# A scan's side work in other slots, and narrower state sums with turned keys in a linear attention

## The chip, the cores and the metric

The kernel runs on one core of one Trainium2 chip. The metric is the device time of one launch in microseconds (us), the median of three runs. One further execution of the same program was taken with the hardware profiler.

## The reference

The kernel computes a four-layer network over 32 sequences of 256 tokens with 128 features (8192 rows). Each layer is an attention-like part and a feed-forward part, both with adaptive layer norm (scale, shift and gate per sequence). Two parts matter here.

Layer 0, a selective scan in two branches (forward and "backward" convolution weights), for the normalized input h:

```python
u = softplus(conv(proj(LN(h))))            # one u per branch
delta = softplus(dt_W @ (deltaBC_W[:64] @ u) + dt_b)
B, C = rows 64..79 and 80..95 of deltaBC_W @ u
h_t = exp(delta_t * A) * h_{t-1} + (delta_t * u_t) * B_t      # 16 states per feature
y_t = sum over states of h_t * C_t, + u_t * D                 # both branches, times silu(proj)
```

Layer 1, an attention with 16 heads of 8 features: a local window of 64 tokens with softmax, and five causal linear attentions (the plain keys and values, and four levels with block means of 2, 4, 8 and 16 tokens), each divided by its normalizer:

```python
phi(x) = elu(x) + 1
out_t = sum over s <= t of phi(q_t) . phi(k_s) v_s / max(sum over s <= t of phi(q_t) . phi(k_s), 1e-6)
```

A gate mixes local and global outputs. Before this part, the routed feed-forward output of layer 0 has to be gathered by token and added to the residual x.

## The kernel before, in words

**Tiles and stages.** `x` stays in SBUF, transposed, as 16 tiles of 128 features by 512 tokens (two sequences). The stages run one after the other: modulation, `scan_layer`, the routed feed-forward of layer 0, `hale` (the attention of layer 1), and five more. Only `scan_layer` and `hale` differ in this change.

**What sets the order.** TensorE's instructions keep the order in which they are written (`mm`, `tr`, L386 and L390), and in the scan ScalarE's do too (`act`, L393, with `strict_act`). VectorE and GpSimd are ordered when the kernel is built, by a scheduler with its own costs; after that each engine takes its queue strictly in that order. What the text calls the built order is the order in which the instructions of the built program stand on an engine.

**The scan.** `scan_layer` writes an agenda of slots. Step p has slots 2p and 2p+1, a tile has eight steps (two branches of four groups of four states), and a tile b has T = 16b. In the first slot, `scan_even` writes 16 products into `dB` (four PSUM banks, one buffer), four scans `hs` on VectorE (L847), the second half of the weighing of step p-2 (products into `y`), the transposes of the first half of step p-1 into `hT`, and two decays (ScalarE exponentials) for step p+1. In the second slot, `scan_odd` has the transposes and the weighing of the other half and two more decays. ScalarE copies every `hT` to `hsT`. All other products and transposes of a tile share the one PSUM bank `tp`: two norms (`norm_rows`, `norm_out`), the projection, the products for u and delta, the rows of B and C (`scan_rows`, with two DMAs on SyncE that turn C through DRAM), the turning of delta times u (`scan_turn`), and the output's turn (`scan_end`). After `scan_end` comes `residual` (L533, two VectorE operations), which waits for two GpSimd products (L912, L913).

**Softplus.** `soft_start` reads a product from PSUM twice: ScalarE makes m = |v + bias|, VectorE r = max(v + bias, 0). `soft_end` makes log(1 + exp(-m)) on ScalarE, and GpSimd adds r. m and r have one buffer each. A tile has four of them (u and delta of both branches).

**The attention of layer 1.** `hale_slots` writes an agenda with 16 slots for a sequence q (T = 16q), which overlaps three sequences. The slots T to T+5 hold the window's six score blocks, T+6 to T+15 the ten blocks of the five linear attentions: scores into `S` (`hale_scores`), a causal mask on VectorE for one half (L1888) and on ScalarE and GpSimd for the other (L1890, L1891), and one slot later the products with the values (`hale_weighted`) into `po`. The second half of a sequence also takes the state of the first half, `kvs`: the sum of keys times values over 128 tokens. `hale_states` makes it by a product of `kt` (keys of the first half, tokens on partitions) with the values (`vzb`, `vzl`; 16 columns for each head: 8 features, then 8 of ones) and a mask for equal heads. `kt` comes from products of its own (a third part of `hale_values`, the key columns in `hale_level_values`) and its own `phi`; the same features, with tokens on the free axis, come from `hale_features` and `hale_level_keys` into `f`. These share three `tp` buffers with the rest.

**The gather.** For a tile that is needed in slot T of an even sequence, `gather_rows` writes eight indirect DMAs on GpSimd's queue (L1239) in slot T-48 and `gather_add` the weighted sums `gy` (L1261, L1262), four transposes and the residual in slot T-38. `got` and `gy` have one buffer.

Of the kernel before, what the change touches and what calls it, by code (L numbers as in the profile page):

```python
# [24 lines left out]
AF = mybir.ActivationFunctionType  # L25
ALU = mybir.AluOpType
# [4 lines left out]
P = 128  # L31
# [144 lines left out]
def packs(d):  # L176

    out = {}
# [40 lines left out]
    k.add("Wv", g["Wv"])  # L219
    k.add("vvk", np.concatenate([g["Wv"].T, g["Wvl"].T, by_heads(g["Wk"].T, DENSE)], 1))  # L220
    k.add("haar_Wk", np.stack([by_heads(diag_blocks(g["haar_Wk"][lvl].T, 16), DENSE) for lvl in range(4)], 1))
# [88 lines left out]
class Program:  # L310
# [326 lines left out]
    def scan_layer(self, w):  # L637
# [7 lines left out]
        with ExitStack() as ctx:  # L645
# [28 lines left out]
            for b in range(NB):  # L674
                a = s[b] = {"b": b}
                T = 16 * b
                put(T, self.clear_regions)

                for o, n, src in ((T - 40, 1, lambda a: self.x[a["b"]]), (T - 32, 2, lambda a: a["h"])):
                    put(o, lambda a, n=n, src=src: a.update({("st", n): self.norm_rows(src(a), self.nc.gpsimd)}), a)  # L680
                    put(o + 1, lambda a, n=n: self.scan_roots(a, n), a)
                    put(o + 3, lambda a, n=n: self.norm_scale(a["st", n][0], *a["r", n]), a)
                put(T - 36, self.scan_norm_out, a)
                put(T - 28, self.scan_norm_out2, s, a)
                put(T - 23, self.scan_proj, s, a)
                put(T - 22, self.scan_gate, s, a)
                put(T - 21, self.scan_gate2, s, a)
                for br in (0, 1):
                    o = T + 8 * br
                    put(o - 18, self.scan_u, s, a, br)  # L690
                    put(o - 17, self.scan_u2, s, a, br)
                    put(o - 15 + br, self.scan_delta, s, a, br)
                    put(o - 14 + br, self.scan_rows, s, a, br)
                    put(o - 11, self.scan_turn, s, a, br)
                    put(o - 9, self.scan_b, s, a, br)
                    put(o - 5, self.scan_c, s, a, br)
                put(T + 18, self.scan_sum, s, a)
                put(T + 19, self.scan_end, s, a)
            for t in sorted(agenda):
# [34 lines left out]
    def soft_start(self, src, bias):  # L734

        m, r = self.wk("sp_m"), self.wk("sp_r")
        self.act(m, src, AF.Abs, bias=bias)
        self.nc.vector.tensor_scalar(r, src, bias, 0.0, ALU.add, ALU.max)
        return m, r

    def soft_end(self, out, m, r):
        self.act(m, m, AF.Exp, scale=-1.0)
        self.act(m, m, AF.Ln, bias=1.0)
        self.nc.gpsimd.tensor_tensor(out, m, r, ALU.add)
# [83 lines left out]
    def scan_even(self, s, p):  # L828

        nc = self.nc  # L830
        if 0 <= p < 8 * NB:
# [13 lines left out]
            for n in range(4):  # L845
                decay = s["decay"][(4 * p + n) % 10].rearrange("p s t -> p (s t)")
                nc.vector.tensor_tensor_scan(hs[:, :, n], decay, dB[:, :, n], 0.0, ALU.mult, ALU.add)  # L847
        self.scan_weigh(s, p - 2, 1)
        self.scan_turned(s, p - 1, 0)
        self.scan_decay(s, p + 1, 0)  # L850

    def scan_odd(self, s, p):
# [46 lines left out]
    def scan_end(self, s, a):  # L899
        nc = self.nc  # L900
        py = self.ps("tp", (P, 4, P))
        for i in range(4):
            self.tr(py[:, i, :], a["yT"][:, i, :])
        y = self.wk("y")
        cut = dict(i=4, r=32)
# [7 lines left out]
        nc.gpsimd.tensor_tensor(y, y, a["h"], ALU.add)  # L913
        self.residual(0, 0, a["b"], y)

# [317 lines left out]

    def gather_rows(self, b):

        got = self.wk("got", (P, 4, 2, P))
        for t in range(4):
            for k in (0, 1):
# [7 lines left out]
                )  # L1246
        self.gather[b] = got

# [295 lines left out]
    def hale(self, w):  # L1544
        nc, c = self.nc, self.c
        BF = mybir.dt.bfloat16
        with ExitStack() as ctx:
# [17 lines left out]
            nc.vector.tensor_copy(self.locb[1], c.locq1)  # L1565
            self.kvs = wk("kvs", (P, 5, SEQ))
            self.kt = wk("kt", (P, 5, P))

# [20 lines left out]
    def hale_slots(self, w):  # L1589
# [9 lines left out]
        for q in range(2 * NB):  # L1599
# [3 lines left out]
            if s == 0:  # L1603
                tiles[b] = {}
                if self.gather:
                    put(side, T - 48, lambda b=b: self.gather_rows(b))
                    put(side, T - 38, lambda b=b: self.gather_add(0, b))
                put(side, T - 32, lambda t=tiles[b], b=b: t.update(xn=self.norm_in(self.x[b])))
                put(side, T - 30, lambda t=tiles[b], b=b: t.update(h=self.norm_out(t["xn"], self.ada_mods(1, 0, b), "h")))
# [18 lines left out]
            put(side, T - 4, lambda a=a: self.hale_features(w, a))  # L1628
            put(side, T - 3, lambda a=a: self.hale_level_values(a, 0, 0))
            put(side, T - 2, lambda a=a: self.hale_level_keys(a, 0))  # L1630
            put(side, T - 2, lambda a=a: self.hale_states(a, (0, 1)))
            put(side, T + 0, lambda a=a: self.hale_level_keys(a, 1))
            put(side, T + 1, lambda a=a: self.hale_level_values(a, 0, 1))
            put(side, T + 2, lambda a=a: self.hale_level_values(a, 1, None))
            put(side, T + 3, lambda a=a: self.hale_states(a, (2, 3)))
            put(side, T + 4, lambda a=a: self.hale_states(a, (4,)))
            for n in range(5):
# [169 lines left out]
    def hale_values(self, w, a, t):  # L1807

        n = 3 if t == 0 else 2
        pv = self.ps("tp", (P, n, P))  # L1810
        self.mm(pv, a["h"][:, t * P : (t + 1) * P], w.vvk[:, 0 : n * P])
        self.nc.vector.tensor_copy(
            self.vzb[t][:, :, :, 0:8], pv[:, 0:2, :].rearrange("p n (h d) -> p n h d", d=8)
        )
        if t == 0:
            self.phi(self.kt[:, 0, :], pv[:, 2, :])

    def hale_level_values(self, a, t, pair):

        if t == 0:  # L1820
            pv = self.ps("tp", (P, 2, 2, P))
            for l in (0, 1):
                lvl = 2 * pair + l
                self.mm(pv[:, l], a["hm"][:, lvl, 0:P], self.wl[:, lvl])
            lv = slice(2 * pair, 2 * pair + 2)
            src = pv[:, :, 1, :]
            self.phi(self.kt[:, 1 + 2 * pair : 3 + 2 * pair, :], pv[:, :, 0, :])
        else:
            src = self.ps("tp", (P, 4, P))
            for lvl in range(4):  # L1830
                self.mm(src[:, lvl, :], a["hm"][:, lvl, P:], self.wl[:, lvl, 1, :])
            lv = slice(0, 4)
        self.nc.vector.tensor_copy(self.vzl[t][:, lv, :, 0:8], src.rearrange("p l (h d) -> p l h d", d=8))

# [26 lines left out]
    def hale_states(self, a, ns):  # L1861

        pk = self.ps("tp", (P, len(ns), SEQ))
        for m, n in enumerate(ns):
            self.mm(pk[:, m, :], self.kt[:, n, :], self.set_values(n, 0)[:, :, 0:16])
        self.nc.vector.tensor_tensor(
            self.kvs[:, ns[0] : ns[-1] + 1, :],
            pk,
            self.c.same.unsqueeze(1).to_broadcast([P, len(ns), SEQ]),
            ALU.mult,  # L1870
        )
# [929 lines left out]
```

## Time and profile before

| | us |
|---|---|
| median of 3 runs (6840.84 to 6861.61) | 6856.3 |
| profiled execution | 6756.19 |
| its span, first to last instruction | 6754.3 |
| busy in the span: TensorE | 5907.4 |
| VectorE | 4350.0 |
| ScalarE | 3557.5 |
| GpSimd | 2660.5 |
| from the first to the last scan instruction (125 to 1144) | 1019 |
| attention of layer 1, first to last score product (1804 to 3826) | 2022 |

The profile is of one execution. In its rows PE is TensorE, PEld its weight loads (which overlap), DVE VectorE, ACT ScalarE, POOL GpSimd, SP SyncE. A row names line, engine and operation, what is written from what, the shape (partitions x elements), and a count; in square brackets a timeline gives the engine's idle time before the row and what ended it. An fp32 product shows as two matmul instructions, called passes here. Lines of helpers (L386, L390, L393, L533) stand for many callers, so one goes by the names of the tiles.

### The profile page before, as it was taken

How to read it: one execution, taken by the hardware profiler on the slowest of the kernel's cores; microseconds unless marked ns; L12 is line 12 of the kernel's file. 1: busy time of each engine (PE TensorE's matmuls, PEld its weight loads, DVE VectorE, ACT ScalarE, POOL GpSimd, SP SyncE). 2: the span in 40 equal slices, each digit the busy share in tenths (PEclk: the TensorE clock that was granted, in tenths of full speed). 3: DMA queues.
4: the chain of work that ended last, by engine and by line, in shares of the span. 5: the costliest groups of instructions: out<-in, count | busy, mean ns of one | idle time of the engine just before them, and what ended most of it. 6: DMA issues, size and time to landing. Idle time of an engine off the chain costs nothing. (4 is left out here: it accounts for less than half of the span.)

```text
span 6754.3 us, 132930 instructions
## 1 busy us (share of the span) xinstructions
PE 5907.4 (87%) x54209; PEld 3313.6 (49%) x54209; DVE 4350.0 (64%) x10025; ACT 3557.5 (53%) x5227; POOL 2660.5 (39%) x2881
## 2 busy tenths in 40 slices
PE   5777776899899999999999887999889998999987
PEld 3555555457555555555566444454422222444444
DVE  3666766621466666666666572888677774777779
ACT  5888885233344444444445442444478886544532
POOL 3555553566444444444444362444244543000000
PEclk7999998899899999999999877999999998989988
DMA  1101101135100000000000101111133442000010
GB/s 60 41 28 41 41 29 36 41 109 134 28 7 5 5 5 8 5 5 8 5 2 2 45 4 38 25 27 28 31 84 90 92 91 48 15 18 18 18 33 30
DMA packets 175447, 232.27 MB, mean 34 GB/s; under 512 B 46519, under 2 KB 95919, under 8 KB 174450
## 3 DMA queue, kind: packets, MB, share of 16 engines
q1 hardware_dynamic: 120656, 124.47, 7.3%
q0 software_dynamic: 26992, 56.62, 3.6%
q10 hardware_dynamic: 27186, 42.67, 1.7%
q8 instruction: 426, 6.98, 0.4%
q14 instruction: 187, 1.53, 0.1%
HBM read 88.28 MB, written 74.97 MB: 24 GB/s over the span
## 5 line engine op out<-in xcount | busy, mean ns | idle before, releaser
L1416 ACT ACTIVATE E<-S 128x1024 f32<-128x1024 f32 x448 | 459.0, 1025 | 592.8 <-PE S L386 579.4
L847 DVE TENSOR_TENSOR_SCAN hs<-decay,dB 128x512 f32<-128x512 f32 x512 | 583.1, 1203 | 196.9 <-PE dB L386 114.7
L298 DVE TENSOR_REDUCE mt<-S 128x4 f32<-128x1024 f32 (+1 forms) x512 | 550.2, 1088 | 224.5 <-PE S L386 223.8
L386 PE MATMUL S<-qa,kx 32*128 32x256 f32 x4096 | 556.2, 392 | 59.6 <-DVE mt L298 59.1
L393 ACT ACTIVATE hid<-S,bigw 128x1024 f32<-128x1024 f32 x512 | 537.6, 1112 | 124.2 <-PE S L386 124.0
L1888 DVE TENSOR_TENSOR E<-S,cst 128x1024 f32<-128x1024 f32 x320 | 391.2, 1223 | 301.1 <-PE S L386 300.5
L1891 POOL TENSOR_SCALAR_AFFINE_SELECT E<-E 128x1024 f32<-128x1024 f32 x320 | 350.2, 1094 | 594.6 <-ACT E L1890 594.2
L386 PE MATMUL S<-kx,q 32*128 32x512 f32 (+1 forms) x2048 | 540.4, 623 | 17.1 <-ACT kx L1534 16.1
L1890 ACT COPY E<-S 128x1024 f32<-128x1024 f32 x320 | 323.7, 1012 | 315.1 <-PE S L386 315.1
L2440 POOL TENSOR_TENSOR acc<-acc,ye 128x512 f32<-128x512 f32 x256 | 344.7, 1347 | 360.4 <-DVE ye L298 318.1
L386 PEld LDWEIGHTS S<-qa,kx 32*128 32x128 f32 x4096 | 350.8, 195 | 174.6 <-DVE mt L298 137.1
L1713 DVE TENSOR_REDUCE mt<-S 128x4 f32<-128x512 f32 (+1 forms) x256 | 205.2, 823 | 294.0 <-PE S L386 293.8
L386 PE MATMUL S<-qG,f 32*128 32x512 f32 x2560 | 382.3, 657 | 7.5 <-DVE E L1888 6.4
L386 PE MATMUL S<-hm,bigw 32*128 32x512 f32 x2048 | 338.7, 654 | 25.2 <-ACT hid L393 25.2
L393 ACT ACTIVATE hsT<-hT 128x1024 f32<-128x1024 f32 x256 | 260.4, 1017 | 179.7 <-PE hT L390 179.4
L390 PE MATMUL hT<-cst,hs 128*128 128x128 f32 x2048 | 285.9, 283 | 75.4 <-ACT hsT L393 73.5
L393 ACT ACTIVATE decay<-dl,A 128x510 f32<-128x510 f32 x512 | 339.2, 714 | 0.0
L386 PE MATMUL po<-E,vzl 128*32 128x128 f32 x8192 | 284.1, 279 | 50.1 <-POOL E L1891 50.1
L1760 ACT ACTIVATE E<-S 128x768 f32<-128x768 f32 (+1 forms) x192 | 169.1, 881 | 280.7 <-PE S L386 279.9
L390 PEld LDWEIGHTS hT<-cst,hs 128*128 128x128 f32 x2048 | 225.1, 143 | 169.6 <-ACT hsT L393 139.7
L386 PE MATMUL po<-E,vz 128*32 128x256 f32 x4096 | 300.2, 379 | 7.2 <-POOL E L1420 6.9
L386 PE MATMUL po<-hid,bigw 128*32 128x512 f32 x2048 | 277.2, 613 | 30.4 <-DVE ye L298 30.4
(520 smaller groups left out, 13307.8 us busy)
## 6 DMA issues: line engine op xcount, KB each, us to landing
gb<-gT SPq DMA_DIRECT2D x256, 256.0 KB
regions<-zeros ACTq DMA_DIRECT2D x16, 2048.0 KB
rx<-far SPq DMA_DIRECT2D x64, 256.0 KB
expert_rows<-eo SPq DMA_DIRECT2D x39, 256.0 KB
out<-out SPq DMA_DIRECT2D x16, 256.0 KB
xTd<-xT SPq DMA_DIRECT2D x15, 256.0 KB
xT<-xTd SPq DMA_DIRECT2D x15, 256.0 KB
bigw<-in_s SPq DMA_DIRECT2D x10, 256.0 KB
```

What stands on the lines that cost most here:

```text
L298: return lambda *args, **kw: self.tc.keep_in_program_order(op(*args, **kw))
L386: return self.tc.keep_in_program_order(self.nc.tensor.matmul(out, lhsT, rhs, start=start, stop=stop, **kw))
L390: return self.tc.keep_in_program_order(self.nc.tensor.transpose(out, in_, self.c.ident[:k, :k]))
L393: ins = self.nc.scalar.activation(*args, **kw)
L847: nc.vector.tensor_tensor_scan(hs[:, :, n], decay, dB[:, :, n], 0.0, ALU.mult, ALU.add)
L1416: nc.scalar.activation(e, src, AF.Exp, scale=scale)
L1713: nc.vector.tensor_reduce(m.rearrange("p (g j) -> p g j", j=2), pm[:, :, x] if i == 0 else pm[:, :, :, 0:192], AX.X, ALU.max, negate=True,)
L1760: nc.scalar.activation(e, src, AF.Exp, scale=1.0 / math.sqrt(8))
L1888: nc.vector.tensor_tensor(e, src, self.c.caus.unsqueeze(1).to_broadcast([P, 8, P]), ALU.mult)
L1890: nc.scalar.copy(e, src)
L1891: nc.gpsimd.affine_select(e, e, [[0, 8], [1, P]], ALU.is_ge, 0.0, base=0, channel_multiplier=-1)
L2440: nc.gpsimd.tensor_tensor(a["acc"], a["acc"], ye, ALU.add)
```

## The change

It has four parts.

1. *Scan, slots.* The four softplus products (`scan_u`, `scan_delta`, for both branches) go to the second slots of steps, with the other users of `tp` placed around them: norms four slots earlier, projection and gate two later, u in slots T-19 and T-13 (was T-18 and T-10), delta in T-15 and T-7 (was T-15 and T-6), the rows in T-14 and T-6, the turn one later, the output two later. The residual leaves `scan_end` and is written in slot T+23 (was T+19). In `scan_even` the transposes and decays come ahead of the weighing.
2. *Scan, softplus.* m no longer comes from ScalarE's Abs: VectorE makes m = v - 2r from r and the product, and ScalarE's Exp adds the bias, so that m + bias = -|v + bias|.
3. *Attention, keys and states.* `kt` is no longer computed from products and `phi`: `hale_turn_keys` transposes the features `f` of the first half (five transposes in two groups, with a ScalarE copy each). The state sums take 9 columns of each head (8 features and one of ones) instead of 16, 144 for 256, in groups of three and two, later. `kvs` is cleared once at the start. The level values of both halves are now made the same way, four products of 128 columns each. The weights lose the key columns.
4. *Gather.* In this stage the rows are fetched in quarters (two DMAs each) in slots T-62, T-58, T-54 and T-50, summed in quarters in T-52 to T-40, and finished in T-38.

```diff
-                for o, n, src in ((T - 40, 1, ...x), (T - 32, 2, ...h)):
+                for o, n, src in ((T - 44, 1, ...x), (T - 36, 2, ...h)):
...
-                put(T - 36, self.scan_norm_out, a)
-                put(T - 28, self.scan_norm_out2, s, a)
-                put(T - 23, self.scan_proj, s, a)
-                put(T - 22, self.scan_gate, s, a)
-                put(T - 21, self.scan_gate2, s, a)
+                put(T - 40, self.scan_norm_out, a)
+                put(T - 32, self.scan_norm_out2, s, a)
+                put(T - 21, self.scan_proj, s, a)
+                put(T - 20, self.scan_gate, s, a)
+                put(T - 19, self.scan_gate2, s, a)
                 for br in (0, 1):
                     o = T + 8 * br
-                    put(o - 18, self.scan_u, s, a, br)
-                    put(o - 17, self.scan_u2, s, a, br)
-                    put(o - 15 + br, self.scan_delta, s, a, br)
-                    put(o - 14 + br, self.scan_rows, s, a, br)
-                    put(o - 11, self.scan_turn, s, a, br)
+                    put(T - 19 + 6 * br, self.scan_u, s, a, br)
+                    put(T - 18 + 6 * br, self.scan_u2, s, a, br)
+                    put(o - 15, self.scan_delta, s, a, br)
+                    put(o - 14, self.scan_rows, s, a, br)
+                    put(o - 10, self.scan_turn, s, a, br)
...
-                put(T + 19, self.scan_end, s, a)
+                put(T + 21, self.scan_end, s, a)
+                put(T + 23, lambda a: self.residual(0, 0, a["b"], a["y"]), a)
...
-        self.act(m, src, AF.Abs, bias=bias)
         self.nc.vector.tensor_scalar(r, src, bias, 0.0, ALU.add, ALU.max)
-        return m, r
+        self.nc.vector.scalar_tensor_tensor(m, r, -2.0, src, ALU.mult, ALU.add)
+        return m, r, bias
-    def soft_end(self, out, m, r):
-        self.act(m, m, AF.Exp, scale=-1.0)
+    def soft_end(self, out, m, r, bias):
+        self.act(m, m, AF.Exp, bias=bias)
...
-        self.scan_weigh(s, p - 2, 1)
         self.scan_turned(s, p - 1, 0)
         self.scan_decay(s, p + 1, 0)
+        self.scan_weigh(s, p - 2, 1)
...
-                    put(side, T - 48, lambda b=b: self.gather_rows(b))
-                    put(side, T - 38, lambda b=b: self.gather_add(0, b))
+                    for t in range(4):
+                        put(side, T - 62 + 4 * t, lambda b=b, t=t: self.gather_rows(b, (t,)))
+                        put(side, T - 52 + 4 * t, lambda b=b, t=t: self.gather_sum(b, (t,)))
+                    put(side, T - 38, lambda b=b: self.gather_end(0, b))
...
-            put(side, T - 3, lambda a=a: self.hale_level_values(a, 0, 0))
-            put(side, T - 2, lambda a=a: self.hale_level_keys(a, 0))
-            put(side, T - 2, lambda a=a: self.hale_states(a, (0, 1)))
-            put(side, T + 0, lambda a=a: self.hale_level_keys(a, 1))
-            put(side, T + 1, lambda a=a: self.hale_level_values(a, 0, 1))
-            put(side, T + 2, lambda a=a: self.hale_level_values(a, 1, None))
-            put(side, T + 3, lambda a=a: self.hale_states(a, (2, 3)))
-            put(side, T + 4, lambda a=a: self.hale_states(a, (4,)))
+            put(side, T - 3, lambda a=a: self.hale_level_keys(a, 0))
+            put(side, T - 2, lambda a=a: self.hale_level_keys(a, 1))
+            put(side, T + 0, lambda a=a: self.hale_level_values(a, 0))
+            put(side, T + 1, lambda a=a: self.hale_turn_keys(a, (0, 1, 2)))
+            put(side, T + 2, lambda a=a: self.hale_level_values(a, 1))
+            put(side, T + 3, lambda a=a: self.hale_turn_keys(a, (3, 4)))
+            put(side, T + 4, lambda a=a: self.hale_states(a, (0, 1, 2)))
+            put(side, T + 5, lambda a=a: self.hale_states(a, (3, 4)))
...
+    def hale_turn_keys(self, a, ns):
+
+        pk = self.ps("tp", (P, len(ns), P))
+        for m, n in enumerate(ns):
+            self.tr(pk[:, m, :], a["f"][:, 1 + n, 0:P])
+        self.nc.scalar.copy(self.kt[:, ns[0] : ns[-1] + 1, :], pk)
...
-        pk = self.ps("tp", (P, len(ns), SEQ))
+        pk = self.ps("tp", (P, len(ns), 16, 9))
         for m, n in enumerate(ns):
-            self.mm(pk[:, m, :], self.kt[:, n, :], self.set_values(n, 0)[:, :, 0:16])
+            self.mm(pk[:, m], self.kt[:, n, :], self.set_values(n, 0)[:, :, 0:9])
```

## The prediction

> **What bounds the kernel now.** I first read the page for the span, then cut the span at the first and last scan instruction and at the first and last score product of the attention stage. Columns: the stretch, its length, then busy us (and instructions) of TensorE, its weight loads, VectorE, ScalarE, GpSimd, then the granted clock.
>
> ```profile
> span 6754.3 us, 132930 instructions
> 125.00:1144.00 1019.00, 779.95 (x10986) 545.27 (x10985) 702.28 (x846) 819.50 (x1343) 536.47 (x630) 0.96 0.11 38
> 1804.00:3826.00 2022.00, 1932.00 (x21905) 1181.76 (x21898) 1257.21 (x2403) 958.70 (x1588) 890.25 (x947) 0.99 0.02 5
> ```
>
> The diff touches these two stretches alone: the scan (1019 us, no engine over 81% busy: a loop of waits) and the attention of layer 1 (2022 us, TensorE busy 95.5%: its own work is the bound). Second, one sequence of the attention: an odd one, the even one after it, and a late odd one that has no rows left to gather.
>
> ```profile
> 1993.67:2063.01 69.34, 63.79 (x705) 38.45 (x701) 43.48 (x92) 31.33 (x54) 33.10 (x36) 0.98 0.04 9
> 2063.01:2124.07 61.06, 60.09 (x692) 36.97 (x688) 37.70 (x65) 29.89 (x50) 25.30 (x28) 1.00 0.01 1
> 3555.57:3618.41 62.84, 61.70 (x705) 38.06 (x701) 41.33 (x84) 31.27 (x54) 25.00 (x28) 1.00 0.01 1
> ```
>
> An even sequence has 1 us of TensorE idle, so there a product saved is time saved. The gather makes an odd one 6.5 us longer. The timeline of TensorE shows where: it waits for a mask by GpSimd, which stands behind six gather DMAs in GpSimd's queue.
>
> ```profile
> 2019.39 0.65 PE L386 MATMUL po<-E,vzl 128*32 128x128 f32 x16
> 2024.21 0.64 PE L386 MATMUL po<-E,vzl 128*32 128x128 f32 x16 [4.17 <-POOL E L1891]
> ...
> 2022.04 1.00 POOL L1239 DMA_INDIRECT got<-expert_rows,back  x1 [0.30 <-issue]
> 2023.05 1.10 POOL L1891 TENSOR_SCALAR_AFFINE_SELECT E<-E 128x1024 f32<-128x1024 f32 x1
> ```
>
> Third, the scan. VectorE runs four scans of a step (4.55 us), then waits until TensorE has filled dB again; dB is one buffer, so this gap can't be hidden. On VectorE's timeline a tile of eight steps takes 64.84 us (574.05 to 638.89): 36.4 of scans and 28.4 of gaps. The gaps ahead of steps 0 to 7 of a tile are 2.43, 3.13, 7.66, 2.28, 2.92, 2.08, 3.56 and 4.34. The largest is the residual's:
>
> ```profile
> 522.29 0.69 DVE L906 TENSOR_TENSOR y<-uu,tp 128x512 f32<-128x512 f32 x1 [0.80 <-PE tp L390]
> 527.69 1.53 DVE L533 SCALAR_TENSOR_TENSOR x<-y,mods,x 128x256 f32<-128x256 f32 x2 [4.71 <-POOL y L913]
> ...
> 523.92 1.28 POOL L912 TENSOR_TENSOR y<-y,z 128x512 f32<-128x512 f32 x1
> 525.15 1.28 POOL L783 TENSOR_TENSOR du<-dl,u 128x512 f32<-128x512 f32 x1
> 526.38 1.28 POOL L913 TENSOR_TENSOR y<-y,h 128x512 f32<-128x512 f32 x1
> ```
>
> VectorE holds the next scans behind the residual, which waits 4.71 us for two GpSimd products with a third between them.
>
> **The change in the scan.** VectorE and GpSimd are ordered when the kernel is built, so I read their built order. The residual is written two slots later, yet in all 15 tiles that have steps left, VectorE's built order is again y, residual, residual, then the scans of the next step. The stall only moves, from the gap ahead of step 2 to that of step 3. There it is: normalization statistics 1.12 (four of 0.85, four of 0.36, overlapped), y 0.69, then GpSimd's y·z, the sum uu (now between, where du was) and y+h, 3 x 1.28 + 0.1, then the residual 1.53: 7.3 us against 7.66. Nothing is won from the name "late".
>
> The softplus loses one ScalarE Abs (0.676 each, four a tile, 2.7 us) and gains one VectorE operation with a PSUM operand. The trace has no such form; the y sum (one PSUM operand, 0.69) and sp_r (PSUM, 0.75) bound it, and I take 0.72. The pair is then 1.45 us long and stands in a gap, beside the dB products: from the start of dB to the first scan it is 1.3 us (products 1.17), so a pair costs little if its own product has ended when the scans end. Behind it are the scans, and behind those everything.
>
> I walked one tile through the built orders with the trace's durations (hsT copy 0.92 and a pair of decays 1.25 from start to start, product of 512 columns 1.0, four transposes 0.55, Exp and Ln 1.25, four scalings 1.6, 0.1 for a handover), from the long stall on, when TensorE and ScalarE have caught up. Gaps ahead of each step:
> 0: 1.35 (2.43), nothing on VectorE, dB can start with the end of the scans.
> 1: 3.4 (3.13); the delta product waits for the bank, which ScalarE frees with xn, behind four scalings and two hsT.
> 2: 3.65 (7.66); the pair waits for GpSimd's dl (1.28), behind Exp and Ln, since sp_m and sp_r are single buffers.
> 3: 7.35 (2.28), the residual.
> 4: 2.3 (2.92); after the stall TensorE has been idle and dB runs at half speed, as it did before one step earlier (2.09 against 1.17).
> 5: 2.3 (2.08), a pair.
> 6: 1.35 (3.56), the pair has gone.
> 7: 4.3 to 5.0 (4.34); ScalarE is busy without a break for 11.3 us through steps 5 and 6 (rows, Exp, Ln, xp, Abs, Exp, Ln, copy), and the u product, then statistics and pair, stand behind it.
> Sum 26.0 to 26.7, so 62.7 us a tile instead of 64.84: 2.1 x 15 = 32 us. The SyncE DMAs of the rows move with their step and have over five steps until their transposes, so they cost nothing; if they were late, TensorE would stand ahead of dB. The other order in a step (transposes ahead of the y products) is in the walk. Bounds for a tile: with the gaps 1, 2 and 7 at half, 5 us less; with the pairs of all four gaps wholly exposed, 4 x 1.45 less the 2.1, some 3.5 us more.
>
> **The change in the attention.** Rows of one even sequence by shape (busy us, mean ns):
>
> ```profile
> L386 PE MATMUL tp<-vzl,kt 128*128 128x256 f32 x8 | 2.3, 392 | 0.0
> L386 PE MATMUL tp<-wl,hm 128*128 128x256 f32 x8 | 2.3, 405 | 0.0
> L386 PE MATMUL tp<-wl,hm 128*128 128x128 f32 x8 | 1.1, 275 | 0.0
> L386 PE MATMUL tp<-w,h 128*128 128x384 f32 x2 | 0.8, 487 | 0.0
> L386 PE MATMUL tp<-w,h 128*128 128x256 f32 x2 | 0.7, 431 | 0.0
> L386 PE MATMUL tp<-vzb,kt 128*128 128x256 f32 x2 | 0.6, 379 | 0.0
> ```
>
> The level values of the first half become eight passes of 128 columns: 2.3 to 1.1. The ten passes of the state sums shrink from 256 to 144 columns: 2.9 to about 1.5 (ten of 0.14). The values lose 0.1. Five transposes come in, 0.16 each by the oc row (3.8 for 24): 0.8. Net 1.9 of busy rows, which overlap: all rows of this sequence add up to 67.5 for 60.1 of union, so 1.7; less 0.25, since a slot that has little beside scores waits 0.3 for VectorE: 1.45 x 32 = 46 us. Here a rule speaks against the row: the Trainium skill (TensorE: Matmul & The Clock Gate, Back-to-back issue gap) says that in a stream of weight loads and matmuls both set the pace, about 81 ns at 128 columns and 131 at 512. Interpolated (an estimate, 98 at 256), narrowing saves a sixth: 0.4 + 0.5 + 0.1 - 0.8, nothing. The rows at 256 and 128 columns with equal loads show a half, so I take the row. Also gone are phi's six short ScalarE operations (2.2 us), for two copies (0.9), and three VectorE ones (1.1), with narrower masks. All lie beside TensorE's work and count nothing.
>
> The gather is written in quarters of two DMAs, four slots apart. But on GpSimd the built order has seven DMAs together, a mask, then the eighth, where it had six, a mask, two. They wait for the sums gy, whose eight operations still stand together on VectorE, as there is one buffer. So the blocked mask comes one DMA later (1.31 us from start to start), less some 0.3 as the kt product ahead of gy has gone: 4.17 becomes about 5.1, behind it the po products. By the skill (same page, The HAM clock gate) TensorE falls to half its clock after some 3.4 us idle; the granted 0.98 here against 1.00 agrees, and that is paid in both. 12 odd sequences x 0.9 = 11 us lost. Were the quarters really spread, the stall's 6.5 x 12 = 78 would be won instead.
>
> **Sum.** 32 + 46 - 11 = 67 off the span of 6754.3: 6687. The profiled execution took 6756.2 with what lies around it; the median 6856.3 of the runs is 100.1 above it. I keep that distance: 6856.3 - 67 = 6789.
>
> **Rivals.** (1) Only the attention gains: the walk is wrong by its 2 us a tile. For it: gaps 1, 2 and 7 hang on chains through three engines. Then 46 - 11 = 35: 6821. (2) The scan gains 5 us a tile, because ScalarE, busiest there, lost 2.7 us: 75 + 35: 6746, or, with gather DMAs in fact spread, some 6700. Against it the built orders. (3) Slower: the pair's wait for GpSimd's dl ahead of step 2. dl stands behind four Cd products (4.07 us), which wait for y products of the tile's last step. In my walk Cd ends just with Ln. If it ends later, every us is a us a tile; from 67/15 = 4.5 us it eats everything, and with 7 us the time is about 6894. Against it: 7 us is a whole step. (4) It doesn't do what it says: stall moved, quarters bunched, narrow passes paced by their loads: 6856 + 11 - 32, about 6835, or no change with the walk wrong too.
>
> **How the numbers follow.** Forecast 0.60 (own range 6750 to 6830), rival 1 0.14, rival 2 0.10, rival 3 0.08, rival 4 0.08. A measurement of this kernel can tell 0.3% (20.6 us) from no change. Faster: 0.60 + 0.12 + 0.10 = 0.82; the same 0.10 (most of rival 4, a little of 1); slower 0.08. Low: scan 5 a tile and half the gather's stall, 6710. High: the rest of rival 3 left out, 6865.
>
> **What would show it.** In the profile after: an even sequence of about 59.6 us and an odd one of 68.5 to 69; seven gather DMAs ahead of a mask with a wait of about 5 us; a scan tile of 62.7 with the residual's wait (near 4 us) ahead of step 3, gaps of 1.35 ahead of 0 and 6. Wrong would be a tile over 65 or under 60, even sequences still at 61, or gather stalls gone.

## The result, and the profile after

| | before | after |
|---|---|---|
| median of the runs compared (five each), us | 6856.3 (6840.84 to 6861.61) | 6786.9 (6771.9 to 6799.81) |
| ratio to before | | 0.990 (0.988 to 0.992) |
| profiled execution, us | 6756.19 | 6771.9 |

The change gains 69 us; 67 were forecast. The two profiled executions say the opposite, because they do not stand alike to their medians: that of before lies 100 us under it, that of after 15. The difference is in stages that the diff leaves alone and whose instructions stand in the same order on VectorE, ScalarE and GpSimd in both profiles: the routed feed-forward of layer 0 took 664 and 686 us, the next mixture of experts 368 and 399, the attention of layer 2 661 and 707. The experiments show such a difference between two chips (below); no chip is named for the two profiles of the result, but that of before fits one of the two chips, and that of after is nearer the other. So only the two changed stages can be compared by profile, and the attention with care. First the page's span; then the windows of the scan, the attention of layer 1, an odd sequence, the even one after it, and a late odd one without a gather (columns as in the prediction: stretch, length, busy us of TensorE, its weight loads, VectorE, ScalarE, GpSimd, granted clock).

```profile
span 6769.9 us, 132928 instructions
```

```profile
127.50:1097.70 970.20, 787.22 (x10982) 559.51 (x10982) 726.50 (x897) 791.94 (x1280) 532.77 (x623) 0.94 0.11 39
1779.40:3767.00 1987.60, 1884.94 (x22057) 1167.20 (x22053) 1172.38 (x2248) 929.46 (x1464) 884.12 (x946) 0.98 0.02 5
2222.04:2291.93 69.89, 63.25 (x709) 38.88 (x705) 40.24 (x87) 30.37 (x50) 32.90 (x35) 0.95 0.04 9
2291.93:2351.49 59.56, 58.59 (x697) 36.44 (x693) 35.16 (x60) 29.00 (x46) 25.16 (x27) 1.00 0.01 2
3503.85:3565.73 61.88, 60.17 (x709) 37.57 (x705) 38.91 (x79) 30.31 (x50) 24.92 (x27) 1.00 0.01 1
```

The scan went from 1019.0 to 970.2 us (49 gained), the attention from 2022.0 to 1987.6 (34 gained here; 22 to 27 between profiles of one chip, see below). Even sequences are 59.56 us as forecast; odd ones with a gather kept almost their whole length.

The residual, on the timelines of VectorE and GpSimd: the stall now stands ahead of step 3, as the built order said.

```profile
580.03 0.65 DVE L908 TENSOR_TENSOR y<-uu,tp 128x512 f32<-128x512 f32 x1
584.53 1.32 DVE L533 SCALAR_TENSOR_TENSOR x<-y,mods,x 128x256 f32<-128x256 f32 x2 [3.85 <-POOL y L915]
585.77 2.32 DVE L849 TENSOR_TENSOR_SCAN hs<-decay,dB 128x512 f32<-128x512 f32 x2
```

```profile
580.77 1.27 POOL L914 TENSOR_TENSOR y<-y,z 128x512 f32<-128x512 f32 x1 [0.34 <-DVE y L908]
582.00 1.27 POOL L788 TENSOR_TENSOR uu<-u 128x512 f32<-128x512 f32 x1
583.22 1.28 POOL L915 TENSOR_TENSOR y<-y,h 128x512 f32<-128x512 f32 x1
```

VectorE waits 3.85 us for two products with `uu` between them, and no scan passes it: all 9929 VectorE instructions start in the same order in this profile and in that of g1, the same program on another occasion. The gather of an odd sequence, GpSimd and then TensorE:

```profile
2250.83 1.04 POOL L1242 DMA_INDIRECT got<-expert_rows,back  x1 [0.30 <-issue]
2251.87 1.11 POOL L1890 TENSOR_SCALAR_AFFINE_SELECT E<-E 128x1024 f32<-128x1024 f32 x1
2253.14 1.27 POOL L1242 DMA_INDIRECT got<-expert_rows,back  x1 [0.16 <-issue]
```

```profile
2253.03 1.08 PE L386 MATMUL po<-E,vzl 128*32 128x128 f32 x16 [4.94 <-POOL E L1890]
2254.05 2.09 PE L386 MATMUL S<-qG,f 32*128 32x512 f32 x8
```

The mask follows the seventh DMA instead of the sixth; TensorE waits 4.94 us, where the profile of before had 4.17, and starts again at half speed (eight score passes take 2.09 us; at the full clock, in e3, 1.14). On one and the same chip the wait grew by 1.3 us, not by these 0.8 (e2 and g1). By shape, an even sequence's changed products:

```profile
L386 PE MATMUL tp<-wl,hm 128*128 128x128 f32 x16 | 2.1, 275 | 0.0
L386 PE MATMUL tp<-vzl,kt 128*128 128x144 f32 x8 | 1.4, 300 | 0.0
L390 PE MATMUL tp<-cst,f 128*128 128x128 f32 x5 | 1.0, 295 | 0.0
L386 PE MATMUL tp<-vzb,kt 128*128 128x144 f32 x2 | 0.4, 289 | 0.0
```

### The profile page after: what moved, and what is told of

Its sections match the earlier page's. It is cut to its first block, busy times and chain, and to the rows that moved or that the text cites. A ratio compares the mean times of both kernels' runs of the same rounds, so it can differ in the third digit from the quotient of the medians.

```text
span 6769.9 us, 132928 instructions
## 1 busy us (share of the span) xinstructions
PE 5927.9 (88%) x54369; PEld 3341.0 (49%) x54369; DVE 4278.6 (63%) x9929; ACT 3493.9 (52%) x5035; POOL 2650.5 (39%) x2882
## 5 line engine op out<-in xcount | busy, mean ns | idle before, releaser
L1422 POOL TENSOR_SCALAR_AFFINE_SELECT E<-E 128x512 f32<-128x512 f32 (+1 forms) x192 | 157.7, 822 | 364.4 <-ACT E L1418 363.9
```

## The experiments

Four kernels ran on one chip, where the kernel before took 6759.4 us (6749.7 to 6772.8), and eight on another, where it took 6872.9 and 6865.5. The difference between the chips lies in the unchanged stages named above (668, 367 and 671 us in e4; 693, 421 and 711 in g1, with the same order there on VectorE, ScalarE and GpSimd). So times are given as ratios to the kernel before on the same chip, and stages are compared by stretch. (e1 to e4 ran on the first chip, the rest on the second.)

### e1: the scan's part alone

```diff
 # the kernel before, with parts 1 and 2 of the change
-                put(T - 23, self.scan_proj, s, a)
+                put(T - 21, self.scan_proj, s, a)
...
-        self.act(m, src, AF.Abs, bias=bias)
+        self.nc.vector.scalar_tensor_tensor(m, r, -2.0, src, ALU.mult, ALU.add)
```

> The scan's part alone (slots, softplus on VectorE, residual in slot T+23), the attention as before. My theory: a scan tile of 62.2 us as in the changed kernel (64.84 before), the scan stretch near 968 us (1017 before), even attention sequences at 61.07 and odd at 69.3 as before; some 45 us less than before in all. The rival that only the attention gains: a scan tile of 64.8, no change in all. A spill-over rival (the attention's gain depends on the scan's part): even sequences below 61.

Measured 0.9939 (0.992 to 0.996), 40 us. The windows of the scan and of the attention:

```profile
128.40:1098.90 970.50, 789.19 (x10982) 561.37 (x10982) 726.68 (x897) 791.81 (x1280) 532.68 (x623) 0.94 0.11 39
1764.50:3785.20 2020.70, 1931.43 (x21902) 1182.39 (x21898) 1256.62 (x2403) 957.24 (x1587) 888.24 (x946) 0.99 0.02 5
```

The scan's whole gain is here, and the attention is that of before. The two stages are independent.

### e2: turned keys and narrow states alone

```diff
 # the kernel before, with part 3 of the change; the gather as before
+            put(side, T + 1, lambda a=a: self.hale_turn_keys(a, (0, 1, 2)))
+            put(side, T + 3, lambda a=a: self.hale_turn_keys(a, (3, 4)))
...
-            self.mm(pk[:, m, :], self.kt[:, n, :], self.set_values(n, 0)[:, :, 0:16])
+            self.mm(pk[:, m], self.kt[:, n, :], self.set_values(n, 0)[:, :, 0:9])
```

> The turned keys and narrow states alone, gather and scan as before. My theory: even sequences at 59.56 us, odd ones at 69.3 (TensorE's saving lost again in the gather stall, which is one DMA longer in this build too, since the built order has seven DMAs ahead of the mask although the gather is written as before); the scan tile 64.84; some 35 us less in all. The rival that the quarters make the stall longer: odd sequences at 67.9, some 50 us less in all.

Measured 0.9971 (0.996 to 0.998), 20 us, where some 35 were expected. An odd sequence and the even one before it:

```profile
2258.27:2328.42 70.15, 62.98 (x709) 38.66 (x709) 39.94 (x87) 30.40 (x49) 33.11 (x35) 0.95 0.04 9
2198.71:2258.27 59.56, 58.59 (x697) 36.44 (x697) 35.16 (x60) 29.02 (x45) 25.17 (x27) 1.00 0.01 1
```

The even sequences have their full gain of 1.5 us. The twelve odd ones with a gather grew: 70.16 us on average, against 69.55 in e1, which has the attention of before and ran on the same chip. TensorE's wait shows why, in e1 and then here:

```profile
2245.97 0.64 PE L386 MATMUL po<-E,vzl 128*32 128x128 f32 x16 [4.17 <-POOL E L1892]
2289.55 1.08 PE L386 MATMUL po<-E,vzl 128*32 128x128 f32 x16 [5.47 <-POOL E L1885]
```

It is longer by 1.30 us, the whole distance from one DMA to the next (1.00 and a pause of 0.30), although the gather is written as before: the built order has seven DMAs ahead of the mask here too. With the gather in quarters (e4, same chip) the wait is 5.46 and the stage, from the first to the last score product, 1993.8 us, against 5.47 and 1993.7 here. So it is the new keys, not the writing in quarters, that let a seventh DMA ahead of the mask. With parts 1 to 3 run apart, 40 + 20 = 60 of the 69 us are found; the rest is within the intervals.

### e3: the gather really spread

In the changed kernel nothing holds a DMA in its slot: the first waits 2.91 us for the last reader of `got`, and six more follow in one block (2242.99 to 2250.83 on GpSimd's timeline). Here each quarter reads its row numbers from a small copy made by GpSimd, and GpSimd's operations of this stage keep their written order, so that a pair of DMAs stands between masks. (Which of the two is needed was not tested.)

```diff
+                row, at = self.wk("row", (P, 2, 1), I32), 0
+                self.nc.gpsimd.tensor_copy(row.bitcast(F), self.back[:, :, 4 * b + t : 4 * b + t + 1].bitcast(F))
...
+            nc.gpsimd.on = True      # keep written order in hale_slots
```

> The changed kernel with the gather really spread: a small GpSimd copy of two row numbers for each quarter, held in the written order with the other GpSimd work of this stage, so that the built order has pairs of DMAs with masks between them. My theory (odd sequences are long by the masks behind seven DMAs): no TensorE idle of 5 us any more, odd sequences at 61.5 to 63 instead of 69.4, some 80 us less than the changed kernel, some 150 less than before. The rival that the 5 us are a wait for something else that only ends with the mask (the rows' landing, the sums): odd sequences stay over 67.

Measured 1.0002 (0.999 to 1.001): all of the change's gain was lost. An odd sequence and the even one after it:

```profile
2019.90:2090.60 70.70, 63.05 (x701) 39.36 (x697) 36.61 (x66) 29.16 (x46) 31.90 (x36) 0.93 0.03 7
1957.90:2019.90 62.00, 60.24 (x709) 37.67 (x705) 40.04 (x81) 30.33 (x50) 27.11 (x30) 1.00 0.01 3
```

The stall left the odd sequence (the second row) and came up in the even one (the first). VectorE's timeline and, in the last row, TensorE's show the new place:

```profile
2042.03 0.85 DVE L1268 TENSOR_SCALAR gy<-got,pair 128x128 f32<-128x128 f32 x1 [3.07 <-DMA got<-expert_rows,row]
2060.22 0.63 DVE L1268 TENSOR_SCALAR gy<-got,pair 128x128 f32<-128x128 f32 x1 [3.92 <-DMA got<-expert_rows,row]
2060.77 1.21 DVE L1894 TENSOR_TENSOR E<-S,cst 128x1024 f32<-128x1024 f32 x1
2062.04 1.33 PE L387 MATMUL S<-qa,k 32*128 32x192 f32 x6 [4.24 <-DVE E L1894]
```

The sum `gy` stands directly behind the issue of its rows and waits for their landing; the mask product `E`, for which TensorE waits, stands behind it. This happens twice in the sequence; TensorE loses 2.05 us behind the first `gy` and 4.24 behind the second, and after that runs at half clock for 10.2 us. A released queue handed its wait to the next one.

### e4: the residual really late

```diff
-                put(T + 23, lambda a: self.residual(0, 0, a["b"], a["y"]), a)
+                put(T + 23, self.scan_residual, a)      # the same, in written order on VectorE
...
+                self.tc.keep_in_program_order(
                 nc.vector.tensor_tensor_scan(hs[:, :, n], decay, dB[:, :, n], 0.0, ALU.mult, ALU.add)
+                )
```

> The changed kernel with the residual really late on VectorE: scans and residual held in the written order, so that the residual stands behind the scans of step 3. My theory: the gap ahead of step 3 falls from 6.7 to about 2 us, the one ahead of step 4 from 2.28 to about 1.6 (TensorE no longer idle before it), the tile from 62.2 to 57 to 58, some 65 us less than the changed kernel. The rival that ScalarE sets the pace: it used the stall to catch up, so the other gaps grow by about as much and the tile stays over 60.5.

Measured 0.9794 (0.978 to 0.981), 139 us under the kernel before, about twice the changed kernel's gain. VectorE in the same step as above, and the scan's window:

```profile
551.12 0.66 DVE L915 TENSOR_TENSOR y<-uu,tp 128x512 f32<-128x512 f32 x1
551.69 4.55 DVE L855 TENSOR_TENSOR_SCAN hs<-decay,dB 128x512 f32<-128x512 f32 x4
556.15 0.98 DVE L298 SCALAR_TENSOR_TENSOR x<-y,mods,x 128x256 f32<-128x256 f32 x2
```

```profile
129.32:1022.67 893.35, 765.41 (x10982) 535.39 (x10982) 720.36 (x897) 790.68 (x1280) 530.52 (x623) 0.98 0.12 43
```

Four scans now stand between `y` and the residual, GpSimd's products end under them, and the gap ahead of step 3 falls from 6.70 to 1.53. That ahead of step 4 falls from 2.28 to 1.36: the `dB` products take 1.17 us there instead of 2.09, and the whole stretch has 20 us at half clock instead of 109. The gap ahead of step 5 grows from 3.08 to 3.83 (median of the middle tiles), the others stay, so a middle tile takes 57.1 us for 62.4. The rival that ScalarE makes up for the gain (over 60.5) did not come true. The stretch is 77 us shorter than after, where some 65 of the time were expected.

### f1, f2: the spread gather with its sums held, and with e4

```diff
 # e3, and in gather_sum:
+        nc.vector.on = len(quarters) == 1     # gy in written order, ten slots behind its DMAs
...
+        nc.vector.on = False
```

> The gather DMAs in pairs, as in e3, and now the weighted sums gy are held on VectorE in the slots in which they are written, ten slots behind their DMAs. Theory (in e3 VectorE stood at gy until the rows had landed, 3.07 us idle, with TensorE's mask product E right behind it): the stall goes for good. Even sequences 59.6 to 60.5, odd ones 61.5 to 62.5, no TensorE wait over 1.5 us, the attention's stretch some 80 us shorter than the changed kernel's 1983, the time about 80 us below the changed kernel, 0.978 of before. Rival (GpSimd's own work is too much: eight DMA issues of 1.0 us, the copies of row numbers and the pauses of 0.3 between them make its masks late wherever the DMAs stand): a sequence with DMAs keeps 68 to 71 us and the time is that of the changed kernel, 0.990, or of e3, 1.000.

> f1 and the late residual of e4 together. Theory (two waits in two stages that share nothing): the gains add up, 80 + 83 below the changed kernel, about 0.966 of before; scan gaps as in e4 (1.5 ahead of step 3), odd sequences 61.5 to 62.5. If f1's theory is wrong: 0.979, as e4.

Measured 0.9938 (0.992 to 0.996) and 0.9833 (0.980 to 0.987): neither better than the same kernel without the spread gather (0.990 and 0.979). f1's windows of the attention of layer 1, and of that of layer 2:

```profile
1783.41:3702.02 1918.61, 1859.49 (x22056) 1158.86 (x22053) 1200.88 (x2256) 928.97 (x1464) 914.04 (x1015) 1.00 0.02 5
```

```profile
4128.30:4916.50 788.20, 707.14 (x5851) 373.00 (x5852) 520.00 (x1493) 291.60 (x380) 252.37 (x334) 0.86 0.09 20
```

In its own stage the theory held: 1919 us, the granted clock 1.00, and only one wait of TensorE over 1.5 us (2.03) in the whole stage. But the attention of layer 2 took 788 us, against 714 in f3 on this chip. Two reasons were possible: a stage that never pauses is paid for by the next, or the edit itself. The last line of the diff also switched off the written order that layer 2 asks for on VectorE, and that stage's order in the trace had changed on VectorE, ScalarE and GpSimd. g2 tells them apart.

### f3, g4: the slots and the softplus apart

```diff
 # f3: the changed kernel with the old softplus (the signs shown); g4: the kernel before with the new one (signs reversed)
+        self.act(m, src, AF.Abs, bias=bias)
-        self.nc.vector.scalar_tensor_tensor(m, r, -2.0, src, ALU.mult, ALU.add)
```

> The changed kernel with the old softplus (ScalarE's Abs, no second VectorE operation) in the new slots. Theory (the slots carry the scan's gain; the softplus trades a ScalarE Abs of 0.68 for a VectorE operation of 0.6 to 0.7 in a gap): the scan's stretch stays within 10 us of 968; the pair gaps (ahead of steps 1, 2, 5, 7) are up to 0.6 shorter where VectorE is late and longer where ScalarE is late, ahead of 2 and 7 above all. Rival (taking work off ScalarE, busiest in the stretch, carries it): the stretch goes back to 1000 or more, 64 us a tile.

> The kernel before with the new softplus alone, in the old slots (which f3's other half leaves: the slots alone took the scan from 1017 to 986). Theory (a ScalarE Abs goes from the chain, a VectorE operation comes into the gap, worth the 18 us that f3 leaves, wherever it stands): scan 995 to 1003. Rival (in the old slots the pair lies ahead of the dB products and is added in full, 4 x 0.7 a tile less what ScalarE gives): the scan stays within 8 us of 1017 or grows; the two parts only work together.

The windows of the scan, f3 and then g4:

```profile
125.83:1114.40 988.57, 784.97 (x10982) 565.46 (x10982) 685.65 (x838) 819.09 (x1339) 532.91 (x623) 0.93 0.11 39
```

```profile
126.45:1145.45 1019.00, 788.39 (x10986) 554.20 (x10985) 730.41 (x905) 795.76 (x1284) 536.98 (x630) 0.94 0.11 38
```

Times 0.9922 (0.989 to 0.995) and 1.0005 (0.999 to 1.002). The slots alone bring 30 of the scan's 49 us, the softplus alone nothing, both together 49: the parts need each other. For f3 both the theory (within 10 us of 968) and the rival (1000 or more) missed; for g4 the rival was right. In g4 ScalarE has 24 us less work, but what the gaps ahead of steps 1 and 7 lose (0.52 and 0.64) the pair adds ahead of steps 0 and 4 (0.80 and 0.28). In the new slots ScalarE is late where the pair is due: with the old softplus the gap ahead of step 5 is 3.87 (3.08 after) and that ahead of step 7 is 4.47 (3.96). Those ahead of 1 and 2 are 3.00 or 3.54, from tile to tile in turn, and 3.31 (3.48 and 3.63).

### f4: wide state sums

```diff
-            put(side, T + 4, lambda a=a: self.hale_states(a, (0, 1, 2)))
+            put(side, T + 4, lambda a=a: self.hale_states(a, (0, 1)))
+            put(side, T + 4, lambda a=a: self.hale_states(a, (2,)))
...
-            self.mm(pk[:, m], self.kt[:, n, :], self.set_values(n, 0)[:, :, 0:9])
+            self.mm(pk[:, m], self.kt[:, n, :], self.set_values(n, 0)[:, :, 0:16])
```

> The changed kernel with state sums of 256 columns (16 of a head) as before, in groups of two, one and two, and the turned keys kept. Theory (an fp32 pass takes time by its columns, 0.29 us at 256 and 0.14 at 144): ten passes give back about 1.3 us a sequence, even sequences 60.8 to 61.0, the attention's stretch and the time some 35 to 42 us longer than the changed kernel's. Rival (a pass with a new weight load is paced by the load[...]): 59.7 to 59.9, and 5 to 8 us in all.

Measured 0.9938 (0.992 to 0.996); g1 on this chip is 0.9899. An even sequence:

```profile
2301.75:2362.23 60.48, 59.51 (x698) 36.96 (x694) 35.88 (x61) 29.03 (x46) 25.20 (x27) 1.00 0.01 2
```

The narrow sums are worth 60.47 - 59.56 = 0.91 us a sequence (medians of the even ones), 0.09 for each of ten passes. That is the difference of the mean durations in the rows by shape (392 ns at 256 columns, 300 at 144). The theory of the row held in kind, with two thirds of the size stated (the stage took 26 us more than g1's, where 35 to 42 were expected); the rival's 59.7 to 59.9 us did not come true.

### g1, g2, g3: the changed kernel again, and the spread gather mended

```diff
 # g2: f1 with the earlier setting restored; g3: g2 and e4
+        held, nc.vector.on = nc.vector.on, nc.vector.on or len(quarters) == 1
...
+        nc.vector.on = held
```

> The changed kernel itself, as the anchor on this chip for the next two: about 0.990 of before, scan stretch 968, attention of layer 1 1983 (even 59.6, odd 68.5 to 70).

> f1 again without its side effect: in f1 the edit also left VectorE of the attention of layer 2 to the scheduler, and that stretch went from 714 (f3, same chip) to 788 us. Now VectorE's built order there is the changed kernel's. Theory (the attention of layer 1 keeps the 69 to 75 us that f1 showed, and the later stretch was lost to its order): the attention of layer 1 1914, of layer 2 as in g1, the time 65 to 80 us below g1. Rival (a stage that runs without pauses is paid for by the next one, whatever its order): the attention of layer 2 again 60 us or more above g1 and the time within 25 us of g1.

> g2 with the late residual of e4. If the gains add: 891 in the scan, 1914 in the attention of layer 1, 140 to 160 us below g1, 0.967 to 0.970 of before. Rival (paid back later): 75 to 90 below g1, 0.979.

| | ratio (interval) | median us | scan | attention 1 | attention 2 |
|---|---|---|---|---|---|
| g1, the change | 0.990 (0.986 to 0.993) | 6793.1 | 969 | 1989 | 711 |
| g2, gather spread | 0.979 (0.975 to 0.983) | 6732.3 | 971 | 1918 | 712 |
| g3, and residual late | 0.969 (0.966 to 0.972) | 6652.2 | 892 | 1918 | 714 |

g1 and g4 also give the gather's wait on this chip, without the new keys (g4) and with them (g1):

```profile
2309.78 1.01 PE L386 MATMUL po<-E,vzl 128*32 128x128 f32 x16 [3.72 <-POOL E L1891]
2259.31 1.08 PE L386 MATMUL po<-E,vzl 128*32 128x128 f32 x16 [5.05 <-POOL E L1890]
```

An odd and an even sequence of g2, and the attention of layer 2:

```profile
2206.59:2268.55 61.96, 60.20 (x710) 37.58 (x706) 39.47 (x81) 30.36 (x50) 27.19 (x30) 1.00 0.02 4
2268.55:2329.24 60.69, 58.67 (x697) 36.45 (x694) 38.00 (x66) 29.02 (x46) 32.12 (x36) 1.00 0.03 8
4117.80:4830.20 712.40, 665.54 (x5853) 358.87 (x5854) 541.68 (x1508) 293.92 (x380) 270.18 (x345) 0.89 0.11 23
```

With the order of layer 2 restored its 788 us are 712 again, so no stage pays for another here: the loss in f1 was the edit's own. (All that follows the attention of layer 1 took 3026 us in g1, 3040 in g2, and also 3040 in f4, which has no spread gather.) In the time g2 gained 61 us on g1, a little under the 65 to 80 expected. With the late residual g3 gained another 80, so the gains add up, and g3 is the fastest kernel of the study, 213 us under the kernel before and 141 under the change.

## Why the prediction was right

**The sum.** 67 forecast, 69 measured. That they are so close is luck in part, for two terms missed in opposite directions. The scan gained 49 us, 17 more than forecast. The attention gained 22 to 27 us between profiles of one chip, 8 to 13 less than forecast; the 34 us between the two profiles of the result come from a pair that seems to differ as the chips do. The scan also starts some 3 us later (at 124.9 us before, 127.5 to 129.3 in the runs with parts 1 and 2), which the sum left out. What is left is within the scatter of the unchanged stages (the routed feed-forward alone took 664 to 672 us in five profiles that fit the first chip). Keeping the 100 us between the profile of before and its median was what made the number comparable.

**The scan, 32 forecast, 49 measured.** The walk itself was good:

| gap ahead of step | 0 | 1 | 2 | 3 | 4 | 5 | 6 | 7 |
|---|---|---|---|---|---|---|---|---|
| forecast | 1.35 | 3.4 | 3.65 | 7.35 | 2.3 | 2.3 | 1.35 | 4.3 to 5.0 |
| measured (median) | 1.36 | 3.48 | 3.63 | 6.70 | 2.28 | 3.08 | 1.45 | 3.96 |

Step 3 was forecast 0.65 too long: the statistics, GpSimd's three products and the residual, put at 1.12, 3.94 and 1.53, take 0.96, 3.73 and 1.24 of the gap, since neighbouring rows overlap. Step 5 was 0.8 too short: VectorE waits 1.34 us there for the softplus product on TensorE (598.50 in the profile after) before it can run the pair. Twelve middle tiles went from 64.85 to 62.4 (2.45 each, forecast 2.1): 29 us. What failed is the step "2.1 x 15": the first tile gained 3.3 and the last three 4.0, 8.2 and 4.1, together 20. Of the 8.2, 5.0 are one gap that only this tile had: 12.6 us ahead of step 2 before, where `y` waited 5.97 for its transposes (1045.44), against 7.66 in the middle tiles. For the rest, little or no side work of a following tile stands in the last tiles, and none of an earlier one in the first; that this is the reason was not tested. The bound of 5 us a tile, of rival 2, was not reached by the middle tiles.

**"The stall only moves."** Right, by the row with 3.85 us. e4 gives the price of the part that did not happen: 77 us.

**The pair costs little.** Right in the whole for the new slots (e1; the pair's second operation took 0.69, forecast 0.72). g4 shows that in the old slots it takes back all that ScalarE's shorter chain gives.

**The attention, 46 - 11 = 35 forecast, 22 to 27 measured on one chip.** Waits are medians; a piece is a stretch of 3.41 us at half clock.

| attention of layer 1 | TensorE's wait | odd sequences with a gather | of these 12, with two pieces | stage, first to last score product |
|---|---|---|---|---|
| first chip, as before (e1) | 4.17 | 69.55 | 3 | 2016.5 |
| first chip, changed (e2, e4) | 5.47, 5.46 | 70.16, 70.19 | 12, 12 | 1993.7, 1993.8 |
| second chip, as before (g4) | 3.73 | 69.31 | 3 | 2011.9 |
| second chip, changed (g1, f3) | 5.05, 5.09 | 69.44, 69.70 | 9, 10 | 1984.9, 1989.6 |
| the result, before | 4.17 | 69.67 | 4 | 2017.7 |
| the result, after | 4.92 | 69.31 | 9 | 1983.2 |

Even sequences gained 1.50 (forecast 1.45), the three late odd ones without a gather 1.17 on average. The twelve with a gather were forecast at about 0.55 less each; on one chip they took 0.1 to 0.6 more. So the seventh DMA cost 16 to 22 us of the gain (12 times 1.17 plus what was added), not 11. Two steps were too simple. The first is "less some 0.3": on both chips the wait grew by a whole DMA, 1.30 and 1.32 us. The forecast of 5.1 looks right beside the 4.9 of the result only because the wait of before beside it, 4.17, is that of the first chip; on the second it is 3.73.

The second is "that is paid in both". The clock records of the traces show what the longer wait adds. All changes of TensorE's clock lie on one grid of 3.413 us (226 changes before, 236 after, none off by more than 0.001 us), so the clock is set window by window, and the windows do not follow the program. Before, the wait of 4.17 us left one window at half clock where it began 1.7 to 3.1 us into a window (8 times), and two where it began in the first 0.7 us or at the very end (4 times). After, the wait of 4.9 left one only where it began 2.2 to 2.3 us into a window (3 times), and two at the other places met (9 times). The wait of 5.47 in e2 always left two. The Trainium skill (TensorE: Matmul & The Clock Gate, The HAM clock gate) says just this, a window of about 3.4 us that runs free of the program; the rule was cited in the prediction, but its length was not carried to the longer wait.

**Row against rule.** The row decided rightly for the narrow sums (f4), though 2.9 us became 1.8 and not 1.5: a pass of 144 columns took 300 ns, and the estimate of 0.14 busy us was that of a pass of 128 (275 ns, 1.1 us for eight).

**The seventh DMA.** Its effect was right in kind, and too small in size; e2 showed that it comes with the keys and would have come without the quarters.

**The rivals.** 1 fell with e1 (the scan gains 49, not 0). 2 fell on the built order, and e3 to g2 show what its spread gather was worth: 71 us of stretch, not 78, and only once a second queue was held too. Its reason for the scan was in part right: with ScalarE's Abs back (f3) 18 of the 49 us are gone, but only the new slots make this relief count (g4). 3 did not occur: VectorE waits for GpSimd's `dl` ahead of step 2, but the gap is 3.63. 4 was right that the residual's stall moves and the quarters bunch, and wrong on the passes.

## What to carry to other kernels

Read the built order before believing that a slot was moved: here a residual "two slots later" only moved its stall by a step, a gather "in quarters" changed nothing, and holding both in place was worth twice the change (141 us on top of 72, g3 and g1). When a wait is taken out of one queue, look at once at which operation of the next queue stands behind the same transfer (e3), and hold that too. Price a stage with its first and last tiles apart from the middle ones. Compare a wait only between profiles of one chip: a forecast that looked exact to 1 us (35 and 34) was off by 8 to 13.

## What was not expected of the hardware

- A wait of TensorE costs more than its length, in steps of one clock window: in the kernel before, a late odd sequence without a gather took 62.84 us; with the wait of 4.17 us and one window at half clock an odd sequence took 69.34, with two windows 70.3. Waits of 3.7 to 4.2 us left two windows in 3 or 4 of 12 sequences, waits of 4.9 to 5.1 in 9 or 10 (7 in f4), waits of 5.47 in all 12.
- The same instructions in the same order (on VectorE, ScalarE and GpSimd) took longer on one chip than on another in the three stages named above: 1707 us in e4 and 1825 in g1 for the three together. The wait of the same six DMAs was the other way round, 4.17 us on the first chip (e1) and 3.73 on the second (g4). No row explains the stages, and it stays open.
- The rows of an indirect DMA reached VectorE 2.7 us after its issue began (2039.34 to 2042.03 in e3), which is long enough to stop an engine whose queue has the reader directly behind it.
